# Sums of a Strassen-Winograd FFN and its residual, moved from GpSimd and VectorE to adding DMA transfers

## Chip, cores and metric

One core of a Trainium2 chip. The metric is the device time of one execution of the kernel in microseconds (us), as a median of several runs. All arithmetic is float32.

## What is computed

One transformer layer on an input of 8 batches x 512 rows x 512 columns: attention, then a feed-forward network (FFN), each with a layer norm ahead of it, one behind it, and a residual. The change touches the FFN alone:

```
x = x + layernorm(attn(layernorm(x)))
h = layernorm(x)
h = fwht(h * SU_ug) / SCALE
x_up   = h @ W_up.T   * (Wscale_ug[:INTER] * SCALE)
x_gate = h @ W_gate.T * (Wscale_ug[INTER:] * SCALE)
h = silu(x_gate) * x_up
h = fwht(h * SU_dp) / SCALE
h = h @ W_down.T * (Wscale_dp * SCALE)
x = x + layernorm(h)
```

`fwht` is a normalised Walsh-Hadamard transform over the last dimension, HIDDEN is 512 and INTER 2048.

## The kernel before

The program is one stream in which the order of every engine's work is written out by hand. Each engine, and each DMA queue, carries out its own instructions in that order and waits on semaphores where another engine's result is needed.

**First half, up to about 930 us.** Attention for all 8 batches, with x after the residual kept in DRAM (`x1d`). The change doesn't touch it.

**Second half.** Batches go in pairs (p = 0 to 3). For a pair, gate and up are computed together by a Strassen-Winograd scheme over 2 x 2 blocks: seven products instead of eight, and then sums of the products. For pair 0 (`seven`, to about 1168 us) the products of gate and of up are made one after the other. For pairs 1 to 3 (`pair` and `deep`) the scheme is used twice: the outer level has seven units in the order 1, 2, 6, 5, 7, 3, 4 (`ORDER`), and each unit is itself seven products of 128 x 128 weights with a 128 x 256 operand (`small(m)`). `pair` runs once for each p = 1, 2, 3 and i = 0 to 7, so 24 times, called "iterations" here.

*A unit (`deep`, L1113 to L1144).* TensorE writes each product into one of four PSUM banks. ScalarE copies products 1 and 5 to SBUF (`m1`, L1132; `m5`, L1136); VectorE adds the others to them (L1133, L1135, L1139, L1141, L1144); GpSimd makes two of the sums (L1140, L1142). `m5` and `u3` have three buffers that take turns. The result is the unit's tile `pr[n]`, 128 partitions x 2 x 512 float32 (512 KB): half 0 is a gate block, half 1 the up block. `copied()` (after L1136) and `place(at)` put other work between: a part of the down projection (`part`, L1225), a silu, a scaling, a step of the next batch's input, or a step of an earlier batch's end.

*The outer sums (`add`, L1345 to L1347).* After a unit, whole tiles `pr` are added to each other. GpSimd makes each such sum as two instructions of 128 x 512. The first sum (2 += 1) is made by VectorE in two instructions (L1375), except at i = 0. The sums are, by the unit after which they stand: 2: 2 += 1; 6: 6 += 1; 5: 5 += 6; 7: 6 += 7 and 7 += 5; 3: 3 += 5; 4: 4 += 6. The finished blocks are c11 (tile 2), c22 (tile 7), c12 (tile 3) and c21 (tile 4).

*Readers of the sums.* ScalarE's silu (L1164) reads half 0, then VectorE's scaling (L1160) reads both halves and writes a block `g` for the down projection. The silu of c11 stands in unit 5 of the same iteration; those of c22, c12 and c21 stand in units 1, 2 and 6 of the next one.

*Reuse of tiles.* There are six `pr` tiles. In the next iteration `pr[1]` is the old `pr[2]`, `pr[2]` the old `pr[5]`, `pr[6]` the old `pr[6]`, `pr[5]` the old `pr[7]`, `pr[7]` the old `pr[3]`, `pr[3]` the old `pr[4]`, and `pr[4]` the tile of the new `pr[1]`. A first write (L1133) to a reused tile waits until all readers of the old contents are through.

*Loads.* SP issues, in one queue, the deep weights (`load_two`, L1057, two 448 KB loads for every two units, asked for four units ahead), the down weights (`wd_load`, L1080, 256 KB, three buffers), the input rows and the stores. In pair 3 the down weights of the last batch are loaded as well (`wd_load_last`, L1093); the last eight of those come after the last iteration.

*The end of a batch (`finish`, L1244 to L1284).* When the 16th block of a batch has been added up, VectorE scales the result (L1250) and the rest goes to a list, `ends`, that `proceed` works off one step at a time: statistics, then for each of four row tiles `close(t)`: ScalarE normalises (L1272), GpSimd adds the residual `x1d` (L1275) from a tile `xres` that SP has loaded (L1259), and SP stores the row (L1276). In units 7 and 4 one `close` is worked off. This is done for batches 0 to 6; batch 7, at the very end, has its own code (`down_rows`, `end_rows`), in which `psz` is the PSUM tile of its down projection.

Of the kernel before, what the change touches and what calls it, by code (L numbers as in the profile page):

```python
# [10 lines left out]
F32 = mybir.dt.float32  # L11
# [3 lines left out]
ALU = mybir.AluOpType  # L15
AX = mybir.AxisListType

P = 128
NB, S, D = 8, 512, 512
# [14 lines left out]
def sandwich_kernel(  # L34
# [19 lines left out]
    nc = tc.nc  # L54
# [10 lines left out]
    x1d = [dram.tile([S, D], F32, name=f"x1d{b}", tag=f"x1d{b}") for b in range(NB)]  # L65
# [31 lines left out]
    def bn(dst, src, name):  # L97
        st = stat.tile([P, 6], F32, tag="st", name=f"st_{name}")
        nc.vector.bn_stats(out=st, in_=src)
        nc.vector.bn_aggr(out=dst, in_=st)  # L100

    def inverse_std(mv, n, name):
        rs = stat.tile([P, NT], F32, tag="rs", name=f"rs_{name}")
        nc.gpsimd.tensor_add(rs[:, :n], mv[:, :n, 1], eps[:, :n])
        nc.gpsimd.tensor_tensor(rs[:, :n], rs[:, :n], nhalf[:, :n], ALU.pow)
        return rs

    def shift_of(mv, rs, n, name):

        sh = stat.tile([P, NT], F32, tag="sh", name=f"sh_{name}")  # L110
        if n == 1:
            nc.vector.tensor_scalar(sh[:, 0:1], mv[:, 0, 0:1], rs[:, 0:1], -1.0, ALU.mult, ALU.mult)
            return sh
        nc.vector.scalar_tensor_tensor(
            sh[:, :n], mv[:, :n, 0], -1.0, rs[:, :n], ALU.mult, ALU.mult
        )
        return sh
# [40 lines left out]
    def in_load(j):  # L158
        b, t = rows[j]
        xrow[j] = room["xin"](f"xin_{b}_{t}")  # L160
        nc.sync.dma_start(out=xrow[j], in_=x1d[b][ts(t, P), :])
# [6 lines left out]
    def in_shift(j):  # L168
        xr_, mv, rs = xrow[j]
        xrow[j] = xr_, rs, shift_of(mv, rs, 1, f"f{j}")  # L170

    def in_norm(j):
        xr_, rs, sh = xrow[j]
        nc.scalar.activation(xr_, xr_, AF.Identity, bias=sh[:, 0:1], scale=rs[:, 0:1])
        xrow[j] = xr_
# [16 lines left out]
    def in_flip(j):  # L192
        ps = room["bank"](f"fxt_{j}").rearrange("p (k q) -> p k q", k=NK)
        for k in range(NK):
            nc.tensor.transpose(ps[:, k, :], xrow[j][:, ts(k, P)], ident)
        xflat[j] = room["flat"](f"xflat_{j}")
        nc.vector.tensor_mul(xflat[j], ps, su.to_broadcast([P, NK, P]))
# [44 lines left out]
    with ExitStack() as actx:  # L242
# [616 lines left out]
        for t in range(NG * NT):  # L859
            n, c = divmod(t, NT)  # L860
            b, i = divmod(t, NK * NT)
# [73 lines left out]
        b = NB - 1  # L935
# [24 lines left out]
        for qc in range(NT):  # L960
            y, rs, sh = ys.pop((b, qc))
# [12 lines left out]
    fs = fctx.enter_context(tc.tile_pool(name="fs", bufs=1, reuse_waits="tile"))  # L974
# [181 lines left out]
    def scale(b, f, c, s):  # L1156

        home = free.pop(0)
        g = fs.tile([P, S], F32, tag=f"g{home}", name=f"g_{b}_{f}")
        nc.vector.scalar_tensor_tensor(g, c, wsu[:, f : f + 1], s, ALU.mult, ALU.mult)  # L1160
        waiting[b].append((f, g, home, now[0]))

    def activate(s, c, f):
        nc.scalar.activation(s, c, AF.Silu, scale=pv[:, C_WSG + f : C_WSG + f + 1])  # L1164
# [80 lines left out]
    def finish(b, t, ps):  # L1245

        if t == 0:
            fy[b] = fs.tile([P, NT, D], F32, tag="fy", name=f"fy_{b}")
        y = fy[b]
        nc.vector.tensor_mul(y[:, t], ps, wsdp_bc)  # L1250
        if t < NT - 1:
            return
        mv = stat.tile([P, NT, 2], F32, tag="mvo", name=f"mvo_{b}", bufs=2)
        r, sr = [], []

        def residuals(t):
            for t in (t, t + 1):
                r.append(fs.tile([P, D], F32, tag=f"xres{t % 2}", name=f"xres_{b}_{t}"))
                nc.sync.dma_start(out=r[t], in_=x1d[b][ts(t, P), :])  # L1259

        def norms(t):
            bn(mv[:, t, :], y[:, t], f"o{b}_{t}")
            if t == NT - 1:
                sr.append(inverse_std(mv, NT, f"o{b}"))
                residuals(0)

        def shift():
            sr.append(shift_of(mv, sr[0], NT, f"o{b}"))

        def close(t):  # L1270
            rs, sh = sr
            nc.scalar.activation(  # L1272
                y[:, t], y[:, t], AF.Identity, bias=sh[:, t : t + 1], scale=rs[:, t : t + 1]
            )
            nc.gpsimd.tensor_add(y[:, t], r[t], y[:, t])  # L1275
            nc.sync.dma_start(out=out[b, ts(t, P), :], in_=y[:, t])  # L1276
            if t == 1:
                residuals(2)

        for t in range(NT):  # L1280
            ends.append(("vector", lambda t=t: norms(t)))
        ends.append(("vector", shift))
        for t in range(NT):
            ends.append(("scalar", lambda t=t: close(t)))  # L1284

    def proceed(by=None):
        if ends and by in (None, ends[0][0]):
            ends.pop(0)[1]()
# [3 lines left out]
    def part():  # L1292
        if not queue:
            queue.extend(down_parts())
        if queue:
            queue.pop(0)()
# [39 lines left out]
    pr = {}  # L1336
    rest_of = {}

    def pair(p, i, inputs):

        bA, bB = 2 * p, 2 * p + 1
        before = dict(rest_of)
        rest_of.clear()

        def add(n, a, b):  # L1345
            for h in range(2):
                nc.gpsimd.tensor_add(pr[n][:, h], pr[a][:, h], pr[b][:, h])  # L1347

        def silu(c, b, f):
            activate(c[:, 0], c[:, 0], f)  # L1350

        def end(c, b, f):
            scale(b, f, c[:, 1], c[:, 0])

        def copied(n):

            if n in (1, 2, 6) and before:
                silu(*before[{1: "c22", 2: "c12", 6: "c21"}[n]])
            elif n == 5:
                silu(pr[2], bA, i)  # L1360
            elif n in (7, 4):
                proceed("scalar")
            for fn in after.pop((n, 0), ()):
                fn()

        def place(n, at):
            if at in PARTS[n]:
                part()
            key = n, at
            if late and key in ((1, 2), (2, 2), (2, 3)):  # L1370
                late.pop(0)()
            elif before and key in ((2, 2), (6, 3), (5, 1)):
                end(*before[{2: "c22", 6: "c12", 5: "c21"}[n]])
            elif key in ((6, 1), (6, 2)) and i > 0:
                nc.vector.tensor_add(pr[2][:, at - 1], pr[2][:, at - 1], pr[1][:, at - 1])  # L1375
            elif key == (7, 1):
                end(pr[2], bA, i)
            elif key in ((1, 2), (7, 2), (4, 2)):
                proceed("vector")
            for fn in after.pop(key, ()):  # L1380
                fn()
            prepare(p, i, n, at)

        after = {}

        def step(n, j, had, last):

            if had:
                in_had(j)
                if j + 2 < last:  # L1390
                    after[n, 3] = [lambda: in_shift(j + 2)]
                if j + 1 < last:
                    after[n, 0] = [lambda: in_norm(j + 1)]
                return
            in_flip(j)
            if j + 3 < last:
                in_load(j + 3)
            if j + 2 < last:
                after[n, 3] = [lambda: in_stats(j + 2)]

        for n in ORDER:
            now[0] += 1
            q = stream.index((p, i, n))
            if q % 2 == 0:
                load_two(q // 2 + 2)
            if n in (2, 5, 3):
                if inputs:
                    step(n, *inputs.pop(0))
            if n == 1:
                new = (  # L1410
                    dict(zip((1, 2, 6, 5, 7, 3), (pr[k] for k in (2, 5, 6, 7, 3, 4))))
                    if pr
                    else {k: pr_tile(f"pr{k}") for k in (1, 2, 6, 5, 7, 3)}
                )
            pr[n] = new.get(n, new[1])
            deep(
                p, i, n, pr[n][:, 0], pr[n][:, 1], lambda n=n: copied(n), lambda at, n=n: place(n, at)
            )
            if n == 2 and i == 0:
                add(2, 2, 1)  # L1420
            elif n == 6:
                add(6, 6, 1)
            elif n == 5:
                add(5, 5, 6)
            elif n == 7:
                add(6, 6, 7)
                add(7, 7, 5)
            elif n == 3:
                add(3, 3, 5)
            elif n == 4:  # L1430
                add(4, 4, 6)
        rest_of.update(c22=(pr[7], bB, i + NH), c12=(pr[3], bB, i), c21=(pr[4], bA, i + NH))


# [75 lines left out]
    b = NB - 1  # L1510
# [104 lines left out]
```

## Time and profile before

| | |
|---|---|
| three runs | 2102.4, 2102.51, 2102.93 us; median 2102.51 |
| the profiled execution | 2102.66 us, of which the span of instructions is 2100.9 us |
| TensorE clock granted | 0.999 of full speed |
| DMA traffic | 218.12 MB, mean 104 GB/s; queue of SP 33.2% of 16 engines' span, queue of GpSimd 0.1% |
| POOL sums of L1347 | 294 instructions, 391.6 us, 1357 ns each |
| POOL residuals L1275 | 28 instructions, 36.1 us, 1293 ns each |
| VectorE sums L1375 | 42 instructions, 28.6 us, 681 ns each |
| loads of `xres` L1259 | 28 of 256 KB, 3.3 us from issue to landing |

Names in the profile: PE is TensorE (PEld its weight loads), DVE VectorE, ACT ScalarE, POOL GpSimd, SP the engine that issues most DMAs; SPq and POOLq are the queues in which those two issue them. A group's line gives the source line, engine, operation, output and inputs, the shape, the count, then busy us and mean ns, then the engine's idle time ahead of these instructions and what ended it. A timeline line begins with the start and the duration in us. The profile's span is shorter than the run's time by 1.8 us.

### The profile page before, as it was taken

The page shows a single profiled execution, that of the slowest core. Times are in us where ns is not written, and L with a number is a line of the kernel's source. Part 1 is how long each engine was busy: PE and PEld are TensorE (multiplying, and loading weights), DVE is VectorE, ACT ScalarE, POOL GpSimd, SP SyncE. Part 2 cuts the span into 40 slices and gives each one's busy share as a digit, 9 for nine tenths or more (in the row PEclk, how much of TensorE's full clock was granted, in tenths as well). Part 3 has the DMA queues.
Part 4 walks back from the last instruction along what each step waited for, and adds up shares of the span by engine and source line. Part 5 has one row for each costly group of instructions (what it writes and reads, how often), then busy time and mean ns, then how long its engine had stood idle before and what let it go on. Part 6 is the DMA issues. An engine that isn't in the chain of part 4 may idle for free.

```text
span 2100.9 us, 26741 instructions
## 1 busy us (share of the span) xinstructions
PE 2076.8 (99%) x9035; PEld 1057.4 (50%) x9042; DVE 1414.4 (67%) x2356; ACT 745.3 (35%) x1199; POOL 1575.4 (75%) x1629
## 2 busy tenths in 40 slices
PE   8999999999999999999999999999999999999998
PEld 4333333333333333344444677676676766777753
DVE  5698777676767677465545866678866678656542
ACT  3554545555555545522121122222222222222211
POOL 4787979787878889645453678788888879787852
PEclk9999999999999999999999999999999999999999
DMA  3112121212121122237454444444343344444432
GB/s 122 37 31 51 42 54 49 47 51 52 46 57 46 32 66 72 70 104 221 145 166 152 146 143 148 133 138 149 130 157 131 131 137 144 138 158 136 138 112 70
DMA packets 215913, 218.12 MB, mean 104 GB/s; under 512 B 87376, under 2 KB 147920, under 8 KB 215776
## 3 DMA queue, kind: packets, MB, share of 16 engines
q1 hardware_dynamic: 215424, 215.32, 33.2%
q8 instruction: 72, 1.18, 0.2%
q0 software_dynamic: 352, 1.08, 0.1%
q14 instruction: 65, 0.53, 0.1%
HBM read 169.18 MB, written 46.92 MB: 103 GB/s over the span
## 4 chain that ended last, share of the span: by engine, by line
PE 94%; DVE 3%; issue 1%; POOL 1%; ACT 1%; DMA 0%; SPq 0%; POOLq 0%; DVEq 0%; ACTq 0%
PE d L1123 24%; PE psy L1225 18%; PE s L527 6%; PE ops L606 6%; PE ps_k L439 5%; PE ps_y L662 5%; PE t L573 5%; PE u L1106 5%; PE g L1106 4%; PE psz L1516 3%; PE t L564 3%; PE l L623 2%; PE ps_q L454 2%; PE ps_v L466 1%; PE ps_cq L407 1%; PE fxh L207 1%
## 5 line engine op out<-in xcount | busy, mean ns | idle before, releaser
L1225 PE MATMUL psy<-wd,g 128*128 128x512 f32 x896 | 448.9, 592 | 0.0
L535 DVE TENSOR_REDUCE nm<-s 128x2 f32<-128x1024 f32 x256 | 300.8, 1216 | 175.1 <-PE s L527 175.1
L1347 POOL TENSOR_TENSOR pr<-pr,pr 128x512 f32<-128x512 f32 x294 | 391.6, 1357 | 9.0
L594 POOL TENSOR_TENSOR p<-p,p 128x512 f32<-128x512 f32 x244 | 330.2, 1384 | 22.1 <-PE ops L606 22.1
L585 ACT ACTIVATE p<-t 128x1024 f32<-128x1024 f32 x256 | 251.8, 1023 | 89.0 <-PE t L573 89.0
L1123 PE MATMUL d<-xb,wq 128*128 128x256 f32 x992 | 254.2, 380 | 1.9 <-DVE inner L1139 1.4
L1123 PEld LDWEIGHTS d<-tt,wq 128*128 128x128 f32 x864 | 164.0, 190 | 144.4 <-issue 106.0
L1123 PE MATMUL d<-tt,wq 128*128 128x256 f32 x864 | 233.8, 379 | 0.2 <-DVE pr L1144 0.2
L1140 POOL TENSOR_TENSOR pr<-inner 128x256 f32<-128x256 f32 x168 | 126.0, 750 | 138.5 <-DVE inner L1139 105.9
L1123 PEld LDWEIGHTS d<-xb,wq 128*128 128x128 f32 x992 | 186.7, 190 | 62.4 <-issue 30.1
L1225 PEld LDWEIGHTS psy<-wd,g 128*128 128x128 f32 x896 | 169.7, 190 | 49.3 <-issue 29.4
L1136 ACT COPY inner<-d 128x256 f32<-128x256 f32 x168 | 62.6, 373 | 309.6 <-PE d L1123 291.5
L1132 ACT COPY inner<-d 128x256 f32<-128x256 f32 x168 | 62.6, 372 | 300.3 <-PE d L1123 193.2
L527 PE MATMUL s<-kT,qT 32*128 32x512 f32 x1024 | 153.8, 639 | 0.7 <-DVE nm L535 0.7
L573 PE MATMUL t<-qT,kT 32*128 32x512 f32 x1024 | 142.8, 598 | 0.0
L606 PE MATMUL ops<-p,v 128*32 128x512 f32 x1024 | 136.8, 605 | 0.0
L1142 POOL TENSOR_TENSOR pr<-pr,inner 128x256 f32<-128x256 f32 x168 | 136.5, 813 | 0.0
L1123 PE MATMUL d<-T,wq 128*128 128x256 f32 x496 | 127.6, 380 | 0.2
L1144 DVE TENSOR_TENSOR pr<-d,inner 128x256 f32<-128x256 f32 x168 | 70.5, 420 | 75.5 <-PE d L1123 72.9
L439 PE MATMUL ps_k<-xT,wkr_sb 128*128 128x512 f32 x256 | 118.3, 605 | 0.7 <-ACT xT L397 0.7
L662 PE MATMUL ps_y<-wo_sb,oT 128*128 128x512 f32 x256 | 115.8, 593 | 0.9 <-DVE oT L657 0.6
L1135 DVE TENSOR_TENSOR inner<-d,inner 128x256 f32<-128x256 f32 x168 | 70.5, 419 | 62.4 <-PE d L1123 62.0
(219 smaller groups left out, 3263.8 us busy)
## 6 DMA issues: line engine op xcount, KB each, us to landing
wq<-wdeep SPq DMA_DIRECT2D x168, 448.0 KB, 4.2
wd<-wdd SPq DMA_DIRECT2D x112, 256.0 KB, 2.8
wdeep<-w SPq DMA_DIRECT2D x32, 448.0 KB, 5.5
xr<-in_x SPq DMA_DIRECT2D x32, 256.0 KB, 2.8
xin<-x1d SPq DMA_DIRECT2D x32, 256.0 KB, 4.0
xres<-x1d SPq DMA_DIRECT2D x32, 256.0 KB, 3.3
out<-fy SPq DMA_DIRECT2D x32, 256.0 KB, 2.0
rec<-rd SPq DMA_DIRECT2D x124, 64.0 KB, 2.0
```

Source lines behind the costliest of these rows:

```text
L439: nc.tensor.matmul(ps, lhsT=wkr_sb[:, k, ts(g, P)], rhs=xT[b][:, k, :], start=(k == 0), stop=(k == NK - 1),)
L527: nc.tensor.matmul(sp[j // 2][:, j % 2, :], lhsT=qT[b][rows, g, ts(qc, P)], rhs=kT[b][rows, g, :], start=True, stop=True,)
L535: nc.vector.tensor_reduce(nms[n][:, qc, 2 * h : 2 * h + 2], sp[h], AX.X, ALU.max, negate=True)
L573: nc.tensor.matmul(sp[j // 2][:, j % 2, :], lhsT=kT[b][rows, g, ts(c, P)], rhs=qT[b][rows, g, :], start=False, stop=True,)
L585: nc.scalar.activation(pt[n, c, h], sp[h], AF.Exp)
L594: nc.gpsimd.tensor_add(into, into, pt[n, c, j // 2][:, j % 2, :])
L606: nc.tensor.matmul(o_ps[n][j * DH : (j + 1) * DH, :], lhsT=vv[b][:, c, ds(g * P + j * DH, DH)], rhs=pt[n, c, j // 2][:, j % 2, :], start=( ...
L662: nc.tensor.matmul(ps, lhsT=oT[b][:, k, ts(qc, P)], rhs=wo_sb[:, k, :], start=False, stop=(k == NK - 1),)
L1106: nc.tensor.matmul(ps, lhsT=w[:, SLOT[n], k, :], rhs=rhs[:, k, :], start=k == 0, stop=k == 1)
L1123: nc.tensor.matmul(ps, lhsT=w[:, INNER[m]], rhs=rhs[m], start=True, stop=True)
L1225: nc.tensor.matmul(ys_[t], lhsT=g[:, ts(t, P)], rhs=w, start=n == 0, stop=n == NI - 1)
L1347: nc.gpsimd.tensor_add(pr[n][:, h], pr[a][:, h], pr[b][:, h])
```

## The change

All seven outer sums of an iteration become one DMA each, issued by GpSimd with `accum_op=ALU.add`: the DMA engines read the source and the destination tile (512 KB) and write the sum. The VectorE form of 2 += 1 goes away. 7 += 5 moves from after unit 7 to after unit 3. The residual of batches 0 to 6 becomes an adding DMA from `x1d` in DRAM straight into `y` (256 KB), issued by GpSimd; the tiles and loads of `xres` go away.

```diff
-        r, sr = [], []
-
-        def residuals(t):
-            for t in (t, t + 1):
-                r.append(fs.tile([P, D], F32, tag=f"xres{t % 2}", name=f"xres_{b}_{t}"))
-                nc.sync.dma_start(out=r[t], in_=x1d[b][ts(t, P), :])
+        sr = []
 
         def norms(t):
             bn(mv[:, t, :], y[:, t], f"o{b}_{t}")
             if t == NT - 1:
                 sr.append(inverse_std(mv, NT, f"o{b}"))
-                residuals(0)
...
-            nc.gpsimd.tensor_add(y[:, t], r[t], y[:, t])
+            nc.gpsimd.dma_start(out=y[:, t], in_=x1d[b][ts(t, P), :], accum_op=ALU.add)
             nc.sync.dma_start(out=out[b, ts(t, P), :], in_=y[:, t])
-            if t == 1:
-                residuals(2)
...
-        def add(n, a, b):
-            for h in range(2):
-                nc.gpsimd.tensor_add(pr[n][:, h], pr[a][:, h], pr[b][:, h])
+        def add(n, a):
+
+            nc.gpsimd.dma_start(out=pr[n], in_=pr[a], accum_op=ALU.add)
...
-            elif key in ((6, 1), (6, 2)) and i > 0:
-                nc.vector.tensor_add(pr[2][:, at - 1], pr[2][:, at - 1], pr[1][:, at - 1])
...
-            if n == 2 and i == 0:
-                add(2, 2, 1)
+            if n == 2:
+                add(2, 1)
             elif n == 6:
-                add(6, 6, 1)
+                add(6, 1)
             elif n == 5:
-                add(5, 5, 6)
+                add(5, 6)
             elif n == 7:
-                add(6, 6, 7)
-                add(7, 7, 5)
+                add(6, 7)
             elif n == 3:
-                add(3, 3, 5)
+                add(7, 5)
+                add(3, 5)
             elif n == 4:
-                add(4, 4, 6)
+                add(4, 6)
```

## Prediction, made before the changed kernel ran

> **What bounds the kernel now.** I read the page's busy table and chain first. The sums that the change moves are the groups of L1347 and L1375.
>
> ```profile
> PE 2076.8 (99%) x9035; PEld 1057.4 (50%) x9042; DVE 1414.4 (67%) x2356; ACT 745.3 (35%) x1199; POOL 1575.4 (75%) x1629
> PE 94%; DVE 3%; issue 1%; POOL 1%; ACT 1%; DMA 0%; SPq 0%; POOLq 0%; DVEq 0%; ACTq 0%
> L1347 POOL TENSOR_TENSOR pr<-pr,pr 128x512 f32<-128x512 f32 x294 | 391.6, 1357 | 9.0
> L1375 DVE TENSOR_TENSOR pr<-pr,pr 128x512 f32<-128x512 f32 x42 | 28.6, 681 | 0.0
> ```
>
> The page's busy line says 99% for PE, and 94% of the chain is PE's. POOL spends 391.6 us and DVE 28.6 us on sums that the change takes away, but neither stands on the chain there. How much PE time can be won back is read stage by stage. The table of stretches (us from the span's start: length, then busy time of PE, PEld, DVE, ACT, POOL, then clock, DMA share, GB/s) covers the 24 pair iterations, 1168 to 2027 us:
>
> ```profile
> 1168.00:1450.00 282.00, 281.90 (x1060) 197.91 (x1059) 200.46 (x422) 72.26 (x161) 227.97 (x241) 1.00 0.41 137
> 1450.00:1490.00 40.00, 38.09 (x141) 25.66 (x140) 37.65 (x67) 9.26 (x21) 39.45 (x35) 1.00 0.43 149
> 1490.00:1735.00 245.00, 244.90 (x924) 172.02 (x923) 167.32 (x353) 64.93 (x145) 201.32 (x214) 1.00 0.41 137
> 1735.00:1775.00 40.00, 39.83 (x148) 27.66 (x147) 36.39 (x66) 9.59 (x22) 39.45 (x35) 1.00 0.43 145
> ```
>
> and this is the longest of TensorE's own waits between 1454 and 1490 us (us in total, times, longest):
>
> ```profile
> PE d L1123 <- DVE inner L1139: 1.4, 2, 0.7
> ```
>
> PE is idle 0.10 + 1.91 + 0.10 + 0.17 = 2.3 us in the whole stage, nearly all of it at 1450 to 1490, where one pair hands over to the next, DVE is busy 37.65 of 40 us and POOL 39.45. The wait says that PE stands for DVE there. So the change can win **at most about 2.3 us**; it can lose far more, since everything that it touches feeds an engine without slack in hand.
>
> **What the Trainium skill says.** (1) "SBUF — State Buffer", section "Who interferes with whom": a VectorE instruction with two SBUF inputs contends with a GpSimd instruction that reads SBUF. The trace agrees: the two-input product of L1160 takes 734 ns at best and 1094 in the median. (2) "DMA: Bandwidth & Descriptors", section "SWDGE vs HWDGE vs iDMA": an accumulating transfer can only be issued by GpSimd, in software. The trace has GpSimd issues without accumulation, 0.56 us each. (3) The same page, "Issuing engines are not separate DMA queues": all run on the same 16 engines. The trace has those engines 41% busy in this stage. (4) "Collectives: The Full Stack", section "The bandwidth ceiling: the fold count and why AG ≠ RS ≠ AR": an adding transfer reads two sources, and the measured rate fell by 1.93. No row of this trace shows one.
>
> **The change part by part.**
> *Removed:* L1347, 294 x 1.357 = 399 us by mean times count (391.6 busy) from POOL; L1375, 42 x 0.681 = 28.6 us from DVE; L1275, 28 x 1.29 = 36 us from POOL; 28 loads of `xres`, 256 KB each, from SP's queue. All of it lies beside PE's work, worth 0 directly. Less contention makes DVE faster at 1450 to 1490. I take 2.0 of the 2.3 us; the ends are 0 and 2.3.
>
> *Added:* 7 x 24 = 168 adding transfers of 512 KB and 28 of 256 KB. The nearest row is the plain store that GpSimd issues:
>
> ```profile
> 924.16 0.65 POOL L964 DMA_DIRECT2D x1d<-y  x1 [0.31 <-POOL y L963]
> q0 software_dynamic: 320, 1.05, 13.5%
> x1d<-y POOLq DMA_DIRECT2D x4, 256.0 KB, 2.3
> ```
>
> Here 1.05 MB took 13.5% of a 20 us window (920 to 940), 2.7 us: 389 GB/s. 256 KB are then 0.68 us of the 2.3 us to landing, so 1.6 us are fixed. 512 KB plain are 1.35 us, with two reads 2.7 us. With 0.3 us between a semaphore and the issue, and an allowance of 0.2 us for more descriptors, an add takes **4.8 us** alone. Bounds: 3.5 us if the second read were free, 6.2 us at three times the plain time (or an equally slower issue).
>
> *POOL* pays about 7 x 0.7 us instead of 12 x 1.36 an iteration, a gain. But an add now **waits in POOL's queue** for the add before it to land: (6,1), (5,6), (6,7), (7,5) are a chain, since each reads or writes a tile of the one before. Behind a waiting issue stand L1140 and L1142 of the next unit; those are waited for through the `m5`/`u3` buffers, three deep, some 10 us: this cover is not the tight one. The tight ones are the readers and the next writers of the sums. I take the iteration at 1868 to 1900 (DVE's L1144 ends a unit, ACT's L1164 is the silu that reads a sum, DVE's L1133 the first write to a reused tile):
>
> ```profile
> 1867.84 0.41 DVE L1144 TENSOR_TENSOR pr<-d,inner 128x256 f32<-128x256 f32 x1
> 1882.84 0.42 DVE L1144 TENSOR_TENSOR pr<-d,inner 128x256 f32<-128x256 f32 x1 [0.87 <-PE d L1123]
> 1890.49 0.73 ACT L1164 ACTIVATE pr<-pr,pv 128x512 f32<-128x512 f32 x1
> 1893.28 0.42 DVE L1133 TENSOR_TENSOR pr<-d,inner 128x256 f32<-128x256 f32 x1 [0.54 <-PE d L1123]
> 1898.02 0.42 DVE L1133 TENSOR_TENSOR pr<-d,inner 128x256 f32<-128x256 f32 x1 [0.48 <-PE d L1123]
> ```
>
> Unit 6 ends at 1868.3. At 4.8 us each: (6,1) starts at 1868.5, when L1142 is through, and lands at 1873.3; (5,6) lands at 1878; (6,7) starts at 1878.6, after the residual's transfer and L1142, and meets the two 448 KB weight loads that SP issues about then, which I charge with 1.8 us: landed at 1885.2. (7,5) lands at 1890.0, (3,5), behind it in the queue, at 1892.7, the residual's 1.35 us later at 1894, (4,6) at about 1897. The readers and writers want them at 1890.49 (7,5), at 1893.28 (both reads of `pr[5]` over, as its tile is the next `pr[2]`) and at 1898.02 ((4,6), whose `pr[6]` is rewritten). **Each is met, by 0.5 to 1 us.** Beyond that, PE itself is ahead by its four PSUM banks: a product's bank is wanted again 4 products and a part later, 4 x 0.43 + 0.86 = 2.6 us, of which the copy uses 0.9: another 1.7 us. Cost in this stage: 0, as long as an add takes less than about 5.5 us with contention counted in the mean.
>
> *DMA engines:* per iteration of 34.9 us (859 us less the ends, over 24) they carry 0.41 x 34.9 = 14.3 us now; added are 7 x 2.7 = 18.9 and about 1.2 x 1.35 = 1.6, removed 1.2 x 0.68 = 0.8: 34.0 us. That is nearly full by the page's own share, in which queued packets count as busy. Weight loads have about four units (20 us) between issue and use, so they can give way.
>
> *SP:* the store of the finished row (L1276) waits for the adding transfer instead of a POOL sum, and SP's later loads queue behind. In the iterations the 20 us of prefetch cover that. At the end they don't:
>
> ```profile
> 2028.66 0.34 SPq L1276 DMA_DIRECT2D out<-fy  x1
> 2029.04 3.77 SPq L1093 DMA_DIRECT2D wdl<-wdd  x8
> 2034.64 5.31 PE L1516 MATMUL psz<-wdl,g 128*128 128x512 f32 x12
> ```
>
> The last eight down weights go out only after that store. By the shift from 1882.84 to this iteration's unit 3 (139.5 us), the residual lands at 2033.5 instead of 2028.6: 4.9 us later. The first load lands 2.9 us after its issue, 2031.9, so 2.7 us are spare: **2.2 us of PE stall**; bounds 0 and 5. The last sum, (4,6), lands at 2036.6 and its product is done by 2038.1; PE wants it at 2039.8: no cost. The rest of the tail has no edit but 4 row sums, 30 us before the end.
>
> **Sum** against the profiled execution (2102.66 us, span 2100.9 and 1.8 around it): -2.0 + 0 + 2.2 = +0.2, so 2102.9; the median of before stands 0.15 below that execution, so I predict **2102.7 us**. The case's own range is 2100 to 2106.5.
>
> **Rivals.** *B, the chain of adds misses its readers (slower).* Place: silu of c22 and the reuse of `pr[5]` and `pr[6]`. It decides once a 512 KB add has over about 3.1 us of data time, or the issue costs 0.5 us more. At 3.3 us the chain is 4 x 0.6 = 2.4 us later, (4,6) lands near 1901 against 1898.02 + 1.7: 1.3 us of stall x 24 = 31, 2134 us; reaching to 2200. For it: margins under 1 us, and 94 to 97% load on the DMA engines. Against it: the measured 1.93 in the skill, and POOL and DVE with more room.
> *C, the DMA engines are the bound.* At 2.5 times plain an iteration needs 7 x 3.38 + 1.2 x 1.7 + 13.5 = 39.2 us against 34.9: +4.3 x 24 = 103, 2206 us; at 3 times 2330. For it: nothing shows the adding rate on this chip's SBUF tiles.
> *D, more is won than PE's idle time shows*, by over 0.2%: 2098. Against it: 24 iterations at full PE rate.
> *E, nothing is freed*: the issue of an adding transfer keeps POOL 2.5 us, as long as the two sums did. POOL would be no worse off, but every link is 1.8 us longer: this ends as B, near 2150.
>
> **Chances.** The forecast case 0.50; B with E 0.28; C 0.18; D 0.04. What a measurement of this kernel can tell from no change is about 0.2%, 4.2 us. Faster 0.04, same 0.50, slower 0.46. The range goes from 2100 to 2210: it leaves out D and most of C.
>
> **What would show it.** Right: PE busy stays above 99% at 1168 to 2027, an add lands in 4 to 5.5 us, POOL's busy time falls by over 300 us, 1450 to 1490 loses its idle time, and the first `psz<-wdl` product waits about 2 us. Wrong: ACT waiting at L1164 or DVE at L1133 on a DMA in every iteration (B), a DMA share near 1 with PE waiting for `wq` or `wd` (C), or long POOL issues (E).

## The result, and the profile after

The changed kernel takes 2177.94 us in the median of four runs (2173.44 to 2189.56), against 2102.72 us for the kernel before, run beside it (2102.4 to 2104.47): a ratio of 1.036 (95% interval 1.032 to 1.041). The profiled execution of the changed kernel took 2173.44 us with a span of 2171.6 us, 70.7 us more than the span before. So the time is **3.6% longer**, where the forecast case was no change.

The first view is the page: the busy times, the chain of work that ended last, and the group of the adding transfers (busy us, mean ns, idle time ahead of it and what ended it).

```profile
PE 2103.3 (97%) x9035; PEld 1067.3 (49%) x9042; DVE 1348.9 (62%) x2314; ACT 746.5 (34%) x1199; POOL 1323.4 (61%) x1503
PE 77%; DMA 12%; issue 4%; DVE 3%; POOL 3%; ACT 1%; DVEq 0%; POOLq 0%; SPq 0%; ACTq 0%
L1339 POOL DMA_DIRECT2D pr<-pr x168 | 148.2, 921 | 225.9 <-DMA pr<-pr 87.4
pr<-pr POOLq DMA_DIRECT2D x168, 512.0 KB, 6.7
```

VectorE and GpSimd have less to do than before, as meant. But PE's part of the chain is 77% where it was 94%, and 12% now belongs to DMA, which had 0%. The last line is the median from issue to landing of an adding transfer: **6.7 us**, where the forecast had 4.8.

The table of stretches shows where the time is lost. The columns are those of the table before (length, busy time of PE, PEld, DVE, ACT and POOL, then clock, DMA share, GB/s); the 24 pair iterations now lie at 1168 to 2090 us.

```profile
1168.00:1455.00 287.00, 276.13 (x1009) 191.26 (x1008) 168.43 (x385) 69.12 (x153) 147.82 (x196) 0.98 0.88 218
1455.00:1500.00 45.00, 41.33 (x147) 28.73 (x145) 31.48 (x66) 9.84 (x22) 23.01 (x27) 0.92 0.89 224
1500.00:1760.00 260.00, 253.35 (x939) 175.65 (x939) 153.25 (x350) 66.36 (x146) 139.63 (x183) 0.99 0.92 227
1760.00:1810.00 50.00, 47.01 (x163) 32.21 (x162) 35.74 (x73) 11.09 (x24) 22.92 (x29) 0.93 0.92 239
1810.00:2090.00 280.00, 261.91 (x949) 181.69 (x948) 136.20 (x313) 61.31 (x138) 129.75 (x166) 0.98 0.89 218
```

The iterations take 922 us instead of 859: **63 us** of the 70.7. PE's idle time there is 922 - 879.7 = 42.3 us; it was 2.3. The other 23 us are PE *busy* time: 879.7 instead of 856.7 us for the same products. The clock column explains nearly all of it: weighted with the lengths, 287 x 0.02 + 45 x 0.08 + 260 x 0.01 + 50 x 0.07 + 280 x 0.02 = 21 us. The remaining 7.7 us lie after the iterations, in the tail.

PE's own waits from 1168 us to the end say for whom it stands (us in total, times, longest):

```profile
PE d L1123 <- DVE pr L1133: 29.3, 20, 3.4
PE d L1123 <- ACT inner L1132: 12.6, 8, 2.9
PE psz L1506 <- DMA wdl<-wdd: 4.4, 1, 4.4
```

and the waits of all engines say what those two stand for:

```profile
ACT pr L1164 <- DMA pr<-pr: 113.0, 50, 6.0
...
POOL pr L1339 <- DMA pr<-pr: 87.4, 33, 4.8
...
DVE pr L1133 <- DMA pr<-pr: 81.1, 29, 6.3
```

The 42 us of PE's idle time are the first two lines of the first view (29.3 + 12.6 = 41.9). VectorE's first write to a reused tile, and ScalarE's silu, wait for adding transfers. L1133 itself empties one of PE's PSUM banks, and behind the silu stands the copy (L1132) that empties another. Followed back one step further in the trace, 28.1 us of PE's idle time lead to the landing of (3,5), the last reader of the tile that unit 2 rewrites, and 10.4 us to that of (7,5). The second line of the second view is the reason that these transfers are late: the issue of an add waits on GpSimd for the add before it.

One iteration (p = 3, i = 2, just before the one that the prediction worked out), seen on GpSimd (start, duration, and the idle time ahead of the instruction with what the profile names for it):

```profile
1879.99 0.88 POOL L1339 DMA_DIRECT2D pr<-pr  x1 [0.30 <-POOL pr L1142]
...
1885.11 0.88 POOL L1339 DMA_DIRECT2D pr<-pr  x1 [1.12 <-DVE pr L1133]
...
1893.31 0.88 POOL L1339 DMA_DIRECT2D pr<-pr  x1 [3.37 <-DVE pr L1141]
...
1899.81 1.77 POOL L1339 DMA_DIRECT2D pr<-pr  x2 [4.19 <-DMA pr<-pr]
```

These are (6,1), (5,6), (6,7), and (7,5) together with (3,5). By the trace (6,1), (5,6), (6,7) and (7,5) take 4.6, 7.6, 6.2 and 5.0 us to land, and each next issue starts 0.3 to 0.6 us after the landing before it. (For the second and third the profile names a VectorE instruction that ends just before the issue. But over the 24 iterations 68 of the 72 issues that follow a link start 0.3 to 0.6 us after its landing, whatever VectorE does, so what comes last is the transfer.) From the first issue to the landing of (7,5) at 1904.8 that is 4.6 + 0.6 + 7.6 + 0.6 + 6.2 + 0.3 + 5.0 = 24.9 us, where the prediction had 21.5 us from 1868.5 to 1890.0. It is much the same in the others: 25.0 us in the median of 24, from 22.0 to 27.8. The readers of this iteration's sums:

```profile
1904.87 0.72 ACT L1164 ACTIVATE pr<-pr,pv 128x512 f32<-128x512 f32 x1 [3.12 <-DMA pr<-pr]
...
1908.73 0.42 DVE L1133 TENSOR_TENSOR pr<-d,inner 128x256 f32<-128x256 f32 x1 [4.82 <-DMA pr<-pr]
...
1909.21 0.70 PE L1123 MATMUL d<-xb,wq 128*128 128x256 f32 x2 [2.60 <-DVE pr L1133]
```

The silu of c22 starts within 0.1 us of the landing of (7,5). The first write of unit 2 to the old `pr[5]` starts after (3,5), the last reader of that tile, has landed at 1908.5. PE stands 2.6 us for it.

In the tail the last down weights come late, as the prediction said:

```profile
2098.14 4.03 SPq L1093 DMA_DIRECT2D wdl<-wdd  x8
...
2101.81 2.08 PE L1506 MATMUL psz<-wdl,g 128*128 128x512 f32 x2 [4.37 <-DMA wdl<-wdd]
```

### The profile page after: what moved, and what is told of

It is laid out like the page before. It is cut to its first block, busy times and chain, and to the rows that moved or that the text cites. A ratio compares the mean times of both kernels' runs of the same rounds, so it can differ in the third digit from the quotient of the medians.

```text
span 2171.6 us, 26801 instructions
## 1 busy us (share of the span) xinstructions
PE 2103.3 (97%) x9035; PEld 1067.3 (49%) x9042; DVE 1348.9 (62%) x2314; ACT 746.5 (34%) x1199; POOL 1323.4 (61%) x1503
## 4 chain that ended last, share of the span: by engine, by line
PE 77%; DMA 12%; issue 4%; DVE 3%; POOL 3%; ACT 1%; DVEq 0%; POOLq 0%; SPq 0%; ACTq 0%
PE d L1123 14%; PE psy L1225 12%; DMA pr<-pr 11%; PE s L527 6%; PE ops L606 6%; PE ps_k L439 5%; PE ps_y L662 5%; PE t L573 5%; PE u L1106 4%; PE g L1106 4%; PE t L564 2%; PE psz L1506 2%; PE l L623 2%; PE ps_q L454 1%; PE ps_v L466 1%
## 5 line engine op out<-in xcount | busy, mean ns | idle before, releaser
L1225 PE MATMUL psy<-wd,g 128*128 128x512 f32 x896 | 455.9, 600 | 0.0
L1123 PE MATMUL d<-xb,wq 128*128 128x256 f32 x992 | 262.2, 387 | 30.3 <-DVE pr L1133 24.7
L1140 POOL TENSOR_TENSOR pr<-inner 128x256 f32<-128x256 f32 x168 | 156.2, 930 | 212.9 <-DVE inner L1139 147.0
L1339 POOL DMA_DIRECT2D pr<-pr x168 | 148.2, 921 | 225.9 <-DMA pr<-pr 87.4
L1142 POOL TENSOR_TENSOR pr<-pr,inner 128x256 f32<-128x256 f32 x168 | 167.9, 1000 | 0.0
L1133 DVE TENSOR_TENSOR pr<-d,inner 128x256 f32<-128x256 f32 x168 | 71.0, 423 | 146.6 <-DMA pr<-pr 81.1
L1132 ACT COPY inner<-d 128x256 f32<-128x256 f32 x168 | 62.1, 369 | 289.0 <-PE d L1123 182.5
L1123 PE MATMUL d<-T,wq 128*128 128x256 f32 x496 | 132.5, 389 | 7.8 <-DVE pr L1133 4.6
L1144 DVE TENSOR_TENSOR pr<-d,inner 128x256 f32<-128x256 f32 x168 | 70.6, 420 | 84.4 <-PE d L1123 83.6
```

Of the source, the lines that this page charges most:

```text
L1123: nc.tensor.matmul(ps, lhsT=w[:, INNER[m]], rhs=rhs[m], start=True, stop=True)
L1142: nc.gpsimd.tensor_add(gate[:, HS:], gate[:, HS:], m5)
L1225: nc.tensor.matmul(ys_[t], lhsT=g[:, ts(t, P)], rhs=w, start=n == 0, stop=n == NI - 1)
```

## The experiments

Two theories stood against each other. **Chain**: an add that needs the one before it cannot be issued until that has landed, so four full landing times stand one after another, and (7,5) and (3,5) at the end miss ScalarE and VectorE. **Engines full**: the DMA engines have too much to carry (their share is 0.88 to 0.92 in the stretches above), whatever the order. Each kernel is timed against the kernel before on the same chip; the times of that lie between 2101.72 and 2101.82 us.

### The two halves of the change

The residual alone: the kernel before, with

```diff
-            nc.gpsimd.tensor_add(y[:, t], r[t], y[:, t])
+            nc.gpsimd.dma_start(out=y[:, t], in_=x1d[b][ts(t, P), :], accum_op=ALU.add)
```

and without the loads of `xres`.

> The kernel before, with only the residual of batches 0 to 6 as an adding transfer. Both theories (late chain of sums, or full DMA engines) put the loss of the pair iterations on the sums: this stays at 2103 to 2107 us, 0 to 4 above the kernel before, and what it loses is lost after the last iteration, where the eight last down weights go out behind a store that waits for the transfer (4.4 us of PE wait there in the changed kernel). If the iterations lose over 10 us here, the residual's transfers or their waits in GpSimd's queue matter and both theories are short of something.

Measured: 2103.49 us, a ratio of 1.0007 (0.9998 to 1.0016). The adding transfer lands in 4.1 us here, and PE doesn't wait at the first `psz<-wdl` product. The sums alone: the changed kernel with the residual as before.

```diff
-            nc.gpsimd.dma_start(out=y[:, t], in_=x1d[b][ts(t, P), :], accum_op=ALU.add)
+            nc.gpsimd.tensor_add(y[:, t], r[t], y[:, t])
```

> The changed kernel with the residual as before (GpSimd sum, loads by SP). Both theories: most of the loss stays, 2160 to 2175 us (changed kernel: 2173 to 2190). The tail's wait for the last down weights goes from 4.4 us to below 2.

Measured: 2169.26 us, a ratio of 1.032 (1.030 to 1.034), with the same three waits (ScalarE 89.6, GpSimd 87.5, VectorE 82.2 us) and transfers that land in 6.5 us. The wait in the tail is 2.7 us, so it is not the residual's alone. It follows that nearly all of the loss belongs to the sums: 67.5 us of it, where the residual alone adds 1.7 us, which can't be told from nothing.

### The same transfers without the chain

All seven transfers stay, at the places where they were, but none follows closely on one that it depends on. The sums are other ones, so this kernel computes something else.

```diff
-                add(5, 6)
+                add(5, 1)
...
-                add(6, 7)
+                add(7, 1)
...
-                add(7, 5)
-                add(3, 5)
+                add(5, 6)
+                add(3, 6)
```

> The changed kernel, with the same number of 512 KB adding transfers at the same places, but onto and from other tiles, so that no transfer waits for the one just before it and every reader has 7 us or more (the sums are other sums than the reference's). Late chain: the waits of L1339 on a transfer (87 us) and of L1133 and L1164 go nearly away, and the time falls to 2105 to 2125 us. Full DMA engines: the traffic is the same, so the time stays at 2160 us or more and the waits on transfers stay.

Measured: 2109.36 us, a ratio of 1.0037 (1.0025 to 1.0049): of the 75.2 us of the changed kernel 7.6 are left (the residual is an adding transfer here as well). Two stretches of it, its group of transfers, and their time to landing:

```profile
1168.00:1455.00 287.00, 286.36 (x1077) 201.17 (x1076) 181.33 (x411) 72.92 (x163) 157.77 (x208) 1.00 0.94 232
...
1500.00:1760.00 260.00, 260.00 (x978) 182.73 (x976) 160.89 (x364) 69.06 (x152) 145.57 (x190) 1.00 0.95 236
```

```profile
L1339 POOL DMA_DIRECT2D pr<-pr x168 | 148.0, 912 | 53.0 <-POOL pr L1142 27.2
...
pr<-pr POOLq DMA_DIRECT2D x168, 512.0 KB, 7.5
```

PE is busy 286.36 of 287 and 260 of 260 us, at the full clock, while the DMA share is 0.94 and 0.95, *higher* than in the changed kernel, and a transfer takes *longer* to land, 7.5 us instead of 6.7. The group no longer waits for a DMA. So full DMA engines by themselves don't stop PE here, and a slow landing doesn't either: this theory falls. What costs is a slow landing that something near waits for. The run takes two such things away at once, the next issue on GpSimd and the early reader behind the last link, and does not tell them apart.

### How much of the chain does it take

Only the four sums of the chain by DMA, (6,1), (5,6), (6,7) and (7,5), the other three as before:

```diff
+    BY_DMA = ((6, 1), (5, 6), (6, 7), (7, 5))
```

> The complement: the four sums of the chain (6 += 1, 5 += 6, 6 += 7, 7 += 5) by adding transfers, 2 += 1 by VectorE, 3 += 5 and 4 += 6 by GpSimd; the residual as before. Late chain: with about half the added traffic each link is about 5.3 to 6 us, so less is lost than with all seven, but it is where the loss is: 2110 to 2150 us. If every adding transfer costs about the same, it is 2140 to 2146 us and e10 2125 to 2135.

Measured: 2121.23 us, a ratio of 1.0092 (1.0074 to 1.0111). The transfers land in 5.5 us, and the chain is seen at once in the group:

```profile
L1348 POOL DMA_DIRECT2D pr<-pr x96 | 84.8, 883 | 188.2 <-DMA pr<-pr 114.5
```

Most of PE's 13.1 us of waits in this run come by other ways than in the changed kernel, though. Only 1.8 us go by the silu. At 1835.3 and 1977.9 us PE stands 1.9 and 1.2 us because VectorE needs row statistics that GpSimd, standing at an issue of the chain, makes late. And 5.9 us lie where one pair hands over to the next: two VectorE instructions take 5.2 and 5.3 us there, which the next run explains in part.

The other three alone, off the chain:

```diff
+    BY_DMA = ((2, 1), (3, 5), (4, 6))
```

> The kernel before, with the three sums that no other sum waits for (2 += 1, 3 += 5, 4 += 6) by adding transfers of 512 KB and the four of the chain by GpSimd; the residual as before. Late chain: each of the three has 8 us or more to its reader, lands in 5 to 6 us, and GpSimd has 5 us less work in an iteration: 2097 to 2102 us, at best below the kernel before. If every adding transfer costs about the same (75 us over 168), it is 2125 to 2135 us.

Measured: 2106.5 us, a ratio of 1.0025 (1.0014 to 1.0036). This was expected a little faster than before, and is 4.7 us slower. ScalarE waits 13.7 us and VectorE 5.9 us for the transfers, which land in 5.9 us; but only one wait of PE, 1.2 us, leads back to a transfer. At 1450 to 1490 us PE is idle 3.8 us where it was 1.9, and there one VectorE instruction takes 2.4 us longer (the kernel before, then this run):

```profile
1459.50 1.62 DVE L237 TENSOR_TENSOR xb<-T,xb 128x1024 f32<-128x1024 f32 x1
1458.64 4.04 DVE L237 TENSOR_TENSOR xb<-T,xb 128x1024 f32<-128x1024 f32 x1
```

PE stands 1.95 us for the instruction behind it, and 1.95 us more at the other hand-over, where L237 takes 4.05 us. In both cases GpSimd has just issued an adding transfer and works without a break on what has queued up behind it; L237 ends 1.1 us after that stretch. So at least part of this cost is not a late sum, but work of GpSimd that comes in one piece and holds up VectorE. Why it does so here, where a stretch of 6.1 us in the kernel before (from 1450.95 us) cost such an instruction 0.5 us, is not shown.

Five of the seven by DMA, with only the first two links of the chain back on GpSimd:

```diff
+    BY_DMA = ((2, 1), (6, 7), (7, 5), (3, 5), (4, 6))
```

> The changed kernel's sums with the residual as before (e2: 2169 us), and the first two links of the chain, 6 += 1 and 5 += 6, made by GpSimd again; the other five sums, 5/7 of the transfers, stay adding transfers at their places. Late chain: 6 += 7 can start as soon as unit 7 is through, two links of 6 us instead of four, so 7 += 5 and 3 += 5 land near their readers: 2105 to 2118 us. If the loss went by the number of transfers, it would be 5/7 of e2's 67: about 2150 us.

Measured: 2114.9 us, a ratio of 1.0063 (1.0040 to 1.0086).

```profile
L1348 POOL DMA_DIRECT2D pr<-pr x120 | 106.1, 941 | 73.7 <-DMA pr<-pr 44.3
...
pr<-pr POOLq DMA_DIRECT2D x120, 512.0 KB, 7.4
```

Two of seven transfers are gone, and with them 54 of the 67.5 us, although a transfer lands no sooner (7.4 us). The load of the DMA engines falls too, to a share of 0.76 to 0.86, so the run alone would not tell the two apart; with the run without a chain it does. The five runs together:

| sums by DMA | longest chain of transfers | slower than before, us |
|---|---|---|
| all seven | 4 | 67.5 |
| all seven, other sums, and the residual | none that waits | 7.6 |
| the chain's four | 4 | 19.4 |
| the other three | none within an iteration | 4.7 |
| five, without (6,1) and (5,6) | 2 | 13.2 |

The chain's four and the other three alone add up to 24.1 us, a good third of what both cost together. The landing times of the chain don't explain the rest: its four links take 5.5 us in the median in both runs, and from the issue of (6,1) to the landing of (7,5) it is 23.9 us alone and 24.4 us beside the other three (medians of 24 iterations). What differs is behind the chain. With all seven by DMA, (3,5) is issued with (7,5) and lands 3.8 us after it, and VectorE stands 82.2 us at L1133 for transfers, 71.3 of them for (3,5). With the chain's four, GpSimd makes (3,5) itself, and VectorE doesn't stand for a transfer at L1133 at all. So a sum that is no link of the chain becomes late by its place behind it. The direct test, all by DMA but (3,5), was not run.

### Smaller pieces

One half of each sum by GpSimd, and one by a transfer of 256 KB:

```diff
-            nc.gpsimd.dma_start(out=pr[n], in_=pr[a], accum_op=ALU.add)
+            nc.gpsimd.tensor_add(pr[n][:, 0], pr[n][:, 0], pr[a][:, 0])
+            nc.gpsimd.dma_start(out=pr[n][:, 1], in_=pr[a][:, 1], accum_op=ALU.add)
```

> The changed kernel's order of sums, with half 0 of each (gate) summed by GpSimd and half 1 (up) by an adding transfer of 256 KB; the residual as before. Late chain: a transfer has half the data, about 1.4 us less alone and 2 to 3 us less beside the loads, lands in 4 to 5 us, and the silu needs none: 2100 to 2108 us. If the fixed part of each transfer or GpSimd's standing at its issues makes the loss, it stays above 2125 us.

Measured: 2111.33 us, a ratio of 1.0043 (1.0029 to 1.0058), some 3 us above what was expected. The transfers land in 4.2 us, and GpSimd waits 13.3 us for them instead of 87.5. With links of 4.2 us the chain is nearly in time, at half of the added traffic; the run doesn't separate the two. PE's own waits, 7.4 us, all lie at the two hand-overs and stand for VectorE.

Only the first sum, (2,1), which VectorE made before:

```diff
-            elif key in ((6, 1), (6, 2)) and i > 0:
-                nc.vector.tensor_add(pr[2][:, at - 1], pr[2][:, at - 1], pr[1][:, at - 1])
...
-            if n == 2 and i == 0:
-                add(2, 2, 1)
+            if n == 2:
+                nc.gpsimd.dma_start(out=pr[2], in_=pr[1], accum_op=ALU.add)
```

> The kernel before, with only the sum 2 += 1 (24 transfers of 512 KB, 7.9 us from issue to the reader, no chain) by an adding transfer instead of 42 VectorE sums. Late chain: no wait, and VectorE has 28 us less work: 2100 to 2102 us, 0 to 2 below the kernel before. If any adding transfer in GpSimd's queue costs, it is 2104 us or more.

Measured: 2101.93 us, a ratio of 1.0002 (0.9994 to 1.0011): nothing that could be told from no change, for a sum whose reader comes two units later.

### What there is to win at most

All outer sums left out of the kernel before, so that it computes something else:

```diff
-            elif n == 6:
-                add(6, 6, 1)
-            elif n == 5:
-                add(5, 5, 6)
...
-            elif n == 4:
-                add(4, 4, 6)
```

> The kernel before with all outer sums left out and nothing in their place, so the outputs are not the reference's: the floor of what any way of making the sums can give. PE idles 2.3 us in the pair iterations of the kernel before: 2099.5 to 2102 us. If it is more than 4 us below the kernel before, more could be won than the idle time of PE showed.

Measured: 2095.89 us, a ratio of 0.9974 (0.9964 to 0.9984): 5.8 us. That is more than the 2.3 us of PE's idle time. Its stretch at 1450 to 1490 us:

```profile
1450.00:1490.00 40.00, 40.00 (x156) 29.03 (x156) 32.93 (x73) 9.52 (x22) 15.80 (x19) 1.00 0.41 139
```

Before, this stretch had 38.09 us busy and 141 instructions of PE. If the 1.91 us of idle time had been all, there would be about 40 / 38.09 x 141 = 148 now; there are 156. (This is rough, as the same 40 us hold a slightly different mix of products.) The ends of units in the two traces are surer: without the sums the program is 0.4 us ahead at 1427 us, 4.4 us at 1497, still 4.4 at 1717, and 5.6 us at 1788 and to the end. So the gain lies at the two hand-overs, 4.0 and 1.2 us, where the idle time was 1.9 and 0.2 us: PE's busy time there hid a part of what was lost. So, with the rest of the kernel as it is, no way of making these sums can win more than 5.8 us (0.3%).

### Giving the chain more time

The readers come later: a seventh `pr` tile, so that unit 2 writes a tile that has been free for longer, the silu of c22 in unit 2 and those of c12 and c21 in unit 6.

```diff
-            if n in (1, 2, 6) and before:
-                silu(*before[{1: "c22", 2: "c12", 6: "c21"}[n]])
+            if n in (2, 6) and before:
+                for c in {2: ("c22",), 6: ("c12", "c21")}[n]:
+                    silu(*before[c])
...
+                    new = dict(zip((1, 2, 6, 5, 7, 3), (pr[2], spare.pop(), pr[5], pr[7], pr[3], pr[4])))
+                    spare.append(pr[6])
```

> The changed kernel with the same sums and transfers, but with a seventh tile, so that the tiles that the sums still read are written one unit or more later, and with the silu of c22 and of c12 one unit (about 5 us) later. Late chain: 5 us more for the readers covers most of the lateness, 2105 to 2130 us, with the chain's own waits in GpSimd's queue still there. Full DMA engines: 2160 us or more, since the same bytes go through the same engines.

Measured: 2140.68 us, a ratio of 1.0184 (1.0164 to 1.0205). Nearly half of the loss goes and the rest stays, so the expectation missed. VectorE no longer waits for an adding transfer at L1133. What is late instead is shown by PE's waits in it:

```profile
PE psy L1225 <- DMA wd<-wdd: 6.9, 2, 3.6
...
PE d L1123 <- DMA wq<-wdeep: 4.0, 3, 2.8
```

Weight loads now come too late: SP stands 260.6 us in its queue at the stores of finished rows, up to 15.4 us at a time, until the adding residual has landed. To test that, each row's store was issued one step later in the list `ends`:

```diff
-            nc.sync.dma_start(out=out[b, ts(t, P), :], in_=y[:, t])
+            held.append(t)
...
+        def close_later(t):
+            store()
+            close(t)
```

> e4 (2141 us), with each finished row's store put one step later in SP's queue, so that SP no longer stands at a store while the adding residual is on its way (261 us of standing in e4's pair iterations, up to 15 us at once, with PE waiting 11 us for down and deep weights). If what e4 has left is SP's standing, this falls to 2105 to 2118 us and PE has no waits for wd or wq. If it is the engines' load or the chain itself, it stays at 2130 to 2142 us.

Measured: 2139.04 us, a ratio of 1.0178 (1.0157 to 1.0199). This lies in the second range, but it doesn't decide: SP still stood 104.1 us at the stores, up to 15.9 us at a time, and PE waited for the weights as before. Then the residual of batches 0 to 6 was left out altogether:

```diff
-            nc.gpsimd.dma_start(out=y[:, t], in_=x1d[b][ts(t, P), :], accum_op=ALU.add)
```

> e4 with the residual of batches 0 to 6 left out altogether (their output lacks it), so that SP's stores wait for ScalarE alone. In e4 and e5 PE waited 11 us for weights whose loads stood behind a store, and stalls are 43 us in all. If the rest of e4 comes from SP standing at stores behind the adding residual, this falls to 2105 to 2118 us with no PE wait on wd or wq. If it comes from the chain, which still makes GpSimd stand at its issues (L1140 and L1142 behind them), it stays at 2125 to 2142 us.

Measured: 2114.78 us, a ratio of 1.0061 (1.0043 to 1.0080). PE's waits for `wq` and `wd` are gone, and 25.9 of the 38.9 us with them. So with later readers the adding residual costs two thirds of what is left, though by itself, in the kernel before, it cost nothing that could be told. Whether by SP's standing or by its own 28 transfers in GpSimd's queue was not separated.

No version that computes the layer was faster than the kernel before.

## Why the prediction was wrong in its main case

The measured 2177.9 us lie inside the range of 2100 to 2210 us, but the range reached so far only because it took in rival B and a price of C. The case that was forecast, 2102.7 us and no loss in the iterations, is off by 75 us, and so is its account of the chain.

**The bound, and what could be won.** That PE bounds the stage was right. "At most about 2.3 us" was too low: without the sums, 5.8 us are won. The sign of the case doesn't depend on it.

**What was removed.** GpSimd's busy time fell by 1575.4 - 1323.4 = 252 us, not by over 300. The sums of 391.6 and 36.1 us did go, but the issues of the adding transfers count as busy, 148.2 us for L1339 alone. An issue takes 0.88 us where 0.7 was taken. Less contention was right: the two-input product of L1160 takes 743 ns in the median instead of 1094, as "SBUF — State Buffer", "Who interferes with whom" in the Trainium skill led one to expect, but the 2.0 us that were counted for it don't show: PE is idle 3.7 us at the first hand-over (1455 to 1500 us), where it was 1.9.

**One add alone.** 4.8 us was right for an undisturbed one: the shortest is 4.5 us in the changed kernel, in the run without a chain, and in the runs with the chain's four or the other three sums. But the median is 5.5 us even with a single sum in an iteration (the run with (2,1) only), with the weight loads in flight beside it. The data time was right as well: GpSimd's queue takes 54.4% of the 922 us of the iterations for 167 sums and 24 residuals, and with the residuals at the forecast's 1.35 us that leaves 2.8 us for a sum, where 2.7 was worked out.

**The chain: the step that failed.** It is "Each is met, by 0.5 to 1 us". Its sum gave each link but one the 4.8 us of an undisturbed add (4.5 us and 0.3 to the next issue), and contention once, 1.8 us at (6,7). Over the 24 iterations a link takes 5.6 us in the median, with 0.3 to 0.6 us to the next issue, so that (7,5) lands 25.0 us after the issue of (6,1), where the sum has 21.5, and (3,5) after 28.4 us, where it has 24.2. The first reader was given 0.5 us to spare. In the iteration shown the weight loads of SP were issued at 1883.7 us, just ahead of (5,6), and that took 7.6 us, 2.8 more than a link was given; the rest of the delay is 0.6 us. The charge of 1.8 us has no working: at the prediction's own 389 GB/s the two loads of 448 KB take 2.4 us, and it was made once in an iteration that has seven such loads. The text had the threshold, "less than about 5.5 us with contention counted in the mean", and close by a load of 34.0 of 34.9 us on the DMA engines; these two numbers were not put together. The runs with several sums by DMA have medians of 5.5 to 7.5 us, by what else is in flight; none stays at 4.8. That one add waits for the landing of the one before, and not for its issue, was right: "DMA: Bandwidth & Descriptors", section "Two DMAs through the same engine are not ordered", in the Trainium skill has the issuing engine wait on the first transfer's semaphore, and the trace has 68 of the 72 issues that follow a link 0.3 to 0.6 us behind its landing.

**PE's cover of 1.7 us** by its PSUM banks was about right: in the iteration shown VectorE stands 4.8 us and PE 2.6, so 2.2 are covered.

**Rival B is what happened**, at the places that it named: the silu of c22, and the reuse of `pr[5]`. It was given 0.28. Its price of 31 us was half of the 63 that the iterations lost. It had 1.3 us of stall an iteration; PE's idle time is 40 / 24 = 1.7 us more than before, and another 21 us come from the lower clock that comes with the stalls, which no step of the prediction had.

**Rival C** is refuted by the run without a chain: the share is 0.94 and 0.95 in its two long stretches, and PE runs at full rate there. The load of 34.0 us was right in size (0.89 x 922 / 24 = 34.2), but the 34.9 us beside it are an iteration of the last pair; over all 24 it is 859 / 24 = 35.8. **Rival E** is refuted by the issue of 0.88 us. **Rival D** had the floor right in its sense (over 0.2% is to be had without the sums), but an adding transfer doesn't reach it.

**SP's cover.** That "20 us of prefetch" cover SP's longer standing held in the changed kernel: 254.0 us at the stores (151.2 before), up to 15.1 us at a time, and no wait of PE for `wq` or `wd`. It holds with little to spare: with later readers it was the next thing to be late.

**The tail.** 2.2 us of stall were forecast with bounds of 0 and 5; it is 4.4 us. The cause given was only a part: with the residual alone there is no stall, with the sums alone 2.7 us. The rest of the 7.7 us is a lower clock there, 0.94.

## What to carry to other kernels

Before a sum on an engine becomes a transfer, count how many such transfers follow on each other and which ones are issued behind them, take the time from issue to landing *under the load that the changed kernel will have* for every link, and compare the whole with the time at which its first reader and the next writer of its tile come. The work that is taken off an engine without a place on the critical path buys nothing, while a transfer's latency is paid by every reader that comes soon. Here the move was free for one sum with a distant reader, cost 4.7 us for three without a chain, and 67.5 us for seven with four in a row.

## What the runs showed of the hardware

- **Stalls of PE are paid twice.** In the run with later readers PE stands 2.44 us at 1537 to 1539.5 us (5 us stretches, columns as above):

```profile
1530.00:1535.00 5.00, 5.00 (x20) 3.62 (x20) 2.21 (x6) 0.75 (x2) 2.85 (x5) 1.00 0.78 150
1535.00:1540.00 5.00, 2.56 (x8) 1.20 (x7) 1.54 (x4) 0.37 (x1) 4.43 (x6) 0.99 1.06 303
1540.00:1545.00 5.00, 5.00 (x15) 3.41 (x14) 2.10 (x7) 1.21 (x3) 3.71 (x5) 0.67 1.03 203
```

  In the next 5 us the granted clock is 0.67, with 15 instructions where a full stretch has 20. "TensorE: Matmul & The Clock Gate", section "Part 1: The HAM clock gate", in the Trainium skill puts this at an idle window of about 3.4 us; here 2.44 us in one piece was enough, and in the changed kernel 2.00 us (1246.7 to 1248.7 us, then 0.70 over 1250 to 1255). It doesn't always come: after the 2.60 us at 1906.6 to 1909.2 us in the changed kernel, and after 3.35 us at 1534.3 us in the run with later readers and no residual, the clock stayed at 1.00. What decides it is not shown. That the stalls bring it, and not the load of the DMA engines, fits the run without a chain (a share of 0.94 and 0.95 at a clock of 1.00), and all eight stretches of lower clock in the changed kernel's iterations, which begin in a stall or within 1 us after one.
- **The adding transfer of 512 KB between SBUF tiles**: 0.88 us of GpSimd for the issue, 4.5 us from issue to landing at best, 6.7 us in the median at a DMA share of 0.9, and an estimated 2.8 us of all 16 engines' time, about twice the 1.35 us that the plain store's rate gives for 512 KB, as the prediction took from its two reads. The median of 6.7 us mixes two kinds: the links of the chain, of which no two are in flight together, take 5.6 us, and the three others, which mostly overlap with another add, 8.6 us. One of 256 KB lands in 3.2 us at best and 4.2 in the median, at a share of 0.7; at that share 512 KB took 4.5 and 5.5 us (the chain's four), so half the data saves 1.3 us.
- **Work of GpSimd in one piece can hold up a VectorE instruction with two inputs in SBUF**: L237 (128 x 1024) took 4.04 and 4.05 us in the run with three sums by DMA and 5.33 us in that with the chain's four, where it takes 1.96 us at most in the pair iterations of the kernel before.
